# Key sums in one chain with one VectorE addition, and the router's rank products issued behind the next tile's transposes

## The chip, the cores and the metric

The kernel runs on one core of a Trainium2 chip (trn2). The time is that of one execution of the whole program on the device, in microseconds; smaller is better. A core has engines that each work through a queue of their own, in order: TensorE (PE; its weight loads are shown as PEld), VectorE (DVE), ScalarE (ACT), GpSimd (POOL) and SyncE (SP), which here only issues transfers. They wait for one another through semaphores. TensorE writes to the PSUM banks, and the other engines read these and the on-chip memory SBUF.

## The reference, cut to what matters

Two layers of gated cross-attention with a mixture of experts behind each. The change touches the router of the first mixture and the softmax of the second attention.

```python
def _L0_ffn_ref(x, router_w, wg, wu, wd):
    logits = jnp.einsum('bsh,eh->bse', x, router_w)
    ...
    idx = jnp.argmax(logits, axis=-1).reshape(-1)
    for e in range(E):
        ...
        out = out + jnp.where((idx == e)[:, None], y, 0.0)
...
def _L1_xattn_ref(query, key_value, Wq, bq, Wk, bk, Wv, bv, Wo, bo):
    scores = jnp.einsum('bhsd,bhtd->bhst', Q, K) * scale
    attn = jax.nn.softmax(scores, axis=-1)
    ctx = jnp.einsum('bhst,bhtd->bhsd', attn, V)
    ...
x = x + jnp.tanh(g_xattn[0]) * _L0_xattn_ref(_layernorm(x, axis=-1), ctx_2048, mask_BxS2_bk0)
x = x + jnp.tanh(g_ffn[0]) * _L0_ffn_ref(_layernorm(x, axis=-1), ...)
x = x + jnp.tanh(g_xattn[1]) * _L1_xattn_ref(_layernorm(x, axis=-1), ctx_2048, ...)
x = x + jnp.tanh(g_ffn[1]) * _L1_ffn_ref(_layernorm(x, axis=-1), ...)
```

Each softmax needs, for every query, the sum of the exponentials over its 1024 keys. Each token of the first mixture goes to one of 8 experts, so a kernel can sort the tokens by expert: it needs each token's expert and its rank among the tokens of that expert.

## The kernel before

The program runs through stages: the first attention with the router (44 to 314 us of the profile), the sorted first mixture (to about 440), the second attention (to about 1256) and the second mixture (to the end). In the stages that the change touches the order of instructions is written out by hand: each engine executes its own in the order of the program's text.

**The router's stage** runs over 16 tiles of 128 tokens, three or four tiles in flight (the loop at line 619). In iteration n, `turn_p(n)` transposes the probabilities of tile n in eight TensorE products, which ScalarE copies out (`a_prT`); `some_weights` prepares a piece of the experts' weights, once or twice per iteration (a `tot` product on TensorE in `weight_scale`, two long VectorE instructions on `w_all`, and two long ScalarE ones); `route_1(n-1)` normalises a row tile for the router; `scores(n+1)`, `turn_x(n+2)`, `softmax(n+1)` and `prepare(n+3)` follow; then `route_3(n-2)` makes the logits (`b_lgp`) and, in a row of small VectorE instructions, the one-hot expert of each token, `oh_all`; `readout(n)` and `finish(n)` close the attention of tile n (`a_o`, and its addition into `x` at line 493); `route_2(n-1)` transposes and quantises the row; and `route_4(n-2)` closes the iteration, before the loads and masks of the next batch. `route_4` (line 561) multiplies `oh_all` with a triangle of ones, and the running sum of earlier one-hots with ones, into one PSUM bank, `b_rkp` (lines 566 and 570): this is each token's rank. GpSimd adds the running sum, five small VectorE instructions from line 586 work out the row's place, and GpSimd issues the scatter of the row (line 595). The bank `lg` is shared by the logits and the rank products.

**The second attention** runs over 16 groups g (4 batches by 4 groups of four heads). A group has U = 16 units t = 16 g + k; unit k is chunk c = k // 2 of 128 keys and pair p = k % 2 of two heads. `score_pairs(t)` does two things at once. For the unit t + 21 it makes scores with queries down the partitions (`c_s`, line 1126), whose maxima VectorE takes (`c_mxn`, line 1143). For unit t it makes transposed scores with the maxima already subtracted (`c_t`, lines 1121 and 1132), which ScalarE exponentiates into a tile `e` (line 1141, 128 keys x 2 heads x 512 queries, nine buffers). The banks for `c_s`, `c_t` and the projections come from one ring of seven. Four units later `weigh` multiplies with the values (`c_o`).

The sum over keys goes three ways. `add_chunks(t)` adds the `e` tiles of one pair element by element, on GpSimd: of the first four chunks into one accumulator, and of the last four into another, so four accumulators and 12 additions per group (chunks 0 and 4 only start a pair, no instruction). `sum_chunks(g, h)` multiplies the two accumulators of half h by ones (four products, line 1209), which gives the sums over the partitions' keys; it is issued eight units after the end of its half, that is in unit 15 of the group for h = 0 and in unit 7 of the next for h = 1. The first half is copied out by ScalarE into `c_rec` (line 1218), and the second is added to it by VectorE (line 1220). `divide` takes reciprocals in four pieces on VectorE and multiplies on GpSimd (`c_oT`, line 1228).

In unit 9 of a group (where `(t + LEAD) % U == 0`) the loop first issues the previous group's `divide`, then in groups 5, 7, 9, 11 and 13 the four row statistics of `ln_part`, then in groups 2, 6 and 10 the queries' projection, and `project_k` (line 1051): sixteen records of TensorE, during which no new scores arise. In unit 10 `split_maxima` reduces the maxima on VectorE (`c_mm`) and splits them into three parts on GpSimd (`c_nm`, `c_pc`); `turn_maxima` transposes these in unit 14. In groups 4, 8 and 12 the values' projection (`c_vp`) comes in unit 4.

Of the kernel before, what the change touches and what calls it, by code (L numbers as in the profile page):

```python
# [14 lines left out]
ALU = mybir.AluOpType  # L15
# [12 lines left out]
def flamingo_kernel(  # L28
# [26 lines left out]
    nc = tc.nc  # L55
# [6 lines left out]
    NM = M // P  # L62
# [115 lines left out]
    NQ = B * NT  # L178
# [122 lines left out]
    with ExitStack() as st:  # L301
# [163 lines left out]
        def turn_p(n):  # L465
            pr = pr_of[n][0]
            prT = wk.tile([P, NM, P], FP, tag="prT", name=f"a_prT_{n}")
            for h in range(NM // 4):
                tp = ps_p.tile([P, 4, P], FP, tag="tp", name=f"a_tp2_{n}_{h}")
                for c in range(4):  # L470
                    nc.tensor.transpose(tp[:, c, :], pr[:, bass.ts(h * 4 + c, P)], ident)
                nc.scalar.copy(prT[:, bass.ts(h, 4), :], tp)  # L472
            prT_of[n] = prT
# [87 lines left out]
        def route_4(n):  # L561

            nonlocal oh_sum
            oh = oh_all[:, n, :]
            rk_ps = ps_1.tile([P, 512], FP, tag="lg", name=f"b_rkp_{n}")
            nc.tensor.matmul(
                rk_ps[:, 0:E], lhsT=earlier, rhs=oh, start=True, stop=(n == 0)
            )
            if n:
                nc.tensor.matmul(  # L570
                    rk_ps[:, 0:E], lhsT=ones_b, rhs=oh_sum, start=False, stop=True
                )
            if n == NQ - 1:
                cnt_ps = rk_ps[:, E : 2 * E]
                nc.tensor.matmul(cnt_ps, lhsT=ones_b, rhs=oh_sum, start=True, stop=False)
                nc.tensor.matmul(cnt_ps, lhsT=ones_b, rhs=oh, start=False, stop=True)
                nc.vector.tensor_copy(cnt, cnt_ps)
            else:
                total = sst.tile([P, E], BF, tag="oh_sum", name=f"b_ohsum_{n}")
                if n:  # L580
                    nc.gpsimd.tensor_tensor(total, oh_sum, oh, ALU.add)
                else:
                    nc.gpsimd.tensor_copy(total, oh)
                oh_sum = total
            mine = sst.tile([P, E], FP, tag="mine", name=f"b_mine_{n}")
            nc.vector.tensor_tensor(mine, rk_ps[:, 0:E], oh, ALU.mult)
            nc.vector.tensor_reduce(rank_all[:, n : n + 1], mine, AX.X, ALU.add)
            place = sst.tile([P, E], FP, tag="place", name=f"b_place_{n}")
            nc.vector.tensor_tensor(place, room_e, oh, ALU.mult)
            plc = sst.tile([P, 1], FP, tag="plc", name=f"b_plc_{n}")  # L590
            nc.vector.tensor_reduce(plc, place, AX.X, ALU.add)
            to = sst.tile([P, 1], U32, tag="to", name=f"b_to_{n}")
            nc.vector.tensor_tensor(to, plc, rank_all[:, n : n + 1], ALU.add)
            row = route_of.pop(n)[1]
            nc.gpsimd.indirect_dma_start(
                out=rows_d[:, :], out_offset=bass.IndirectOffsetOnAxis(ap=to[:, :], axis=0),
                in_=row[:, :], in_offset=None,
            )
# [19 lines left out]
        h = 0  # L618
        for n in range(-2, NQ):
            if 0 <= n < NQ:  # L620
                turn_p(n)
            if n >= 0:
                some_weights(h)
                h += 1
            if 0 <= n - 1 < NQ:
                route_1(n - 1)
            if 0 <= n + 1 < NQ:
                scores(n + 1)
            if n + 2 < NQ:
                turn_x(n + 2)  # L630
            if n == -2:
                for q in range(4):
                    weight_load(q, nc.scalar)
                nc.scalar.activation(gates, graw, AF.Tanh)
                nc.scalar.preload_act_table_set("natural_log_exp_and_others")
            if n == -1:
                set_valid(0)
            if 0 <= n + 1 < NQ:
                softmax(n + 1)
            if n + 3 < NQ:  # L640
                prepare(n + 3)
            if n >= 0 and n % 4 != 3:
                some_weights(h)
                h += 1
            if n == NQ - 1:
                break
            if 0 <= n - 2 < NQ:
                route_3(n - 2)
            if 0 <= n < NQ:
                finish(n, readout(n))  # L650
            if 0 <= n - 1 < NQ:
                route_2(n - 1)
            if 0 <= n - 2 < NQ:
                route_4(n - 2)
            if n >= -1 and (n + 5) % NT == 0 and n + 5 < NQ:
                load_x((n + 5) // NT)
                load_memT((n + 5) // NT)
                load_mem((n + 5) // NT)
            if n >= 0 and (n + 4) % NT == 0 and n + 4 < NQ:
                set_mask((n + 4) // NT)  # L660
            if n >= 0 and (n + 3) % NT == 0 and n + 3 < NQ:
                set_valid((n + 3) // NT)

        n = NQ - 1
# [22 lines left out]
        acc_all = memp.tile([P, 4, 2, S], FP, tag="mem", name="c_acc")  # L687
# [267 lines left out]
    with ExitStack() as st:  # L955
# [22 lines left out]
        NG = B * NK  # L978
        U = 16
# [9 lines left out]
        for i in range(2):  # L989
            t = big.tile([P, NT, 4, HD], BF, tag=f"pc{i}", name=f"c_pc_{i}")  # L990
# [5 lines left out]
        mxn_of, mT_of, e_of, acc_of, ou_of, rec_of = {}, {}, {}, {}, {}, {}  # L996
# [171 lines left out]
        def weigh(g, c, h):  # L1168
# [10 lines left out]
            if c == NM - 1 and h == 1:  # L1179
                ou_of[g] = wk.tile([P, S], FP, tag="ou", name=f"c_ou_{g}", bufs=1)  # L1180
                nc.scalar.copy(ou_of[g], o_bank)  # L1181

        def add_chunks(t):

            g, k = divmod(t, U)
            c, p = divmod(k, 2)
            if c % 4 == 0 or (g == NG - 1 and c >= NM - 2):
                return

            eng = nc.vector if g == NG - 1 and t % 2 else nc.gpsimd  # L1190
            if c % 4 == 1:
                acc = acc_all[:, (2 * (c // 4) + p) % 4]
                acc_of[g, c // 4, p] = acc
                eng.tensor_tensor(acc, e_of[t - 2], e_of[t], ALU.add)  # L1194
            else:
                acc = acc_of[g, c // 4, p]
                eng.tensor_tensor(acc, acc, e_of[t], ALU.add)  # L1197

        def sum_chunks(g, h):
            ps = ps_s.tile([P, S], FP, tag="s", name=f"c_sum_{g}_{h}")  # L1200
            terms = [(acc_of[g, h, 0], acc_of[g, h, 1])]
            if g == NG - 1 and h == 1:

                terms += [
                    (e_of[g * U + 2 * c], e_of[g * U + 2 * c + 1]) for c in (NM - 2, NM - 1)
                ]
            for n, term in enumerate(terms):
                for i in range(4):
                    nc.tensor.matmul(  # L1209
                        ps[i * HD : (i + 1) * HD, :], lhsT=ones[:, 0:HD],  # L1210
                        rhs=term[i // 2][:, i % 2, :],
                        start=(n == 0), stop=(n == len(terms) - 1),
                    )
            if h == 1 and g == NG - 1:
                return ps
            if h == 0:
                rec_of[g] = wk.tile([P, S], FP, tag="rec", name=f"c_rec_{g}", bufs=1)
                nc.scalar.copy(rec_of[g], ps)
            else:
                nc.vector.tensor_tensor(rec_of[g], rec_of[g], ps, ALU.add)  # L1220

        def divide(g, q):
            rq = rec_of[g][:, bass.ts(q, P)]
            nc.vector.reciprocal(rq, rq)
            if q == NT - 1:
                oT = big.tile([P, S], FP, tag="oT", name=f"c_oT_{g}", bufs=5)
                eng = nc.vector if g == NG - 2 else nc.gpsimd
                eng.tensor_tensor(oT, ou_of.pop(g), rec_of[g], ALU.mult)
                oT_of[g] = oT
# [123 lines left out]
        for t in range(-LEAD, NG * U + LAG):  # L1353

            for j in range(NT):
                d = t + LEAD + NT + 1 - j
# [3 lines left out]
                d = t + LEAD + NT - j  # L1360
                if d % (NK * U) == 0 and 1 <= d // (NK * U) < B:
                    turn_q(d // (NK * U), j)
            if (t + LEAD) % U == 0 and 0 <= t + LEAD < NG * U:
                g = (t + LEAD) // U
                if g >= NK:
                    for q in range(NT):
                        divide((t - 24) // U, q)
                if t in stats_at:
                    tag, b = stats_at[t]
                    for j in range(NT):  # L1370
                        ln_part(b, j, tag)
                if g % NK == 0:
                    project_q(g // NK)
                if g >= NK:
                    project_k(g, 0)
                    project_k(g, 1)
# [51 lines left out]
                b, j = divmod(d, NT)  # L1428
                tp_of[d] = turn_d(ps_s, "s", b, j, xn_of.pop((b, j)), None)
            d = t - 2 * LAG  # L1430
            if 0 <= d < NG * U - 1 and d % 8 == 7:
                sum_chunks(d // U, d % U // 8)

            if (t + LEAD) % (NK * U) == (NK - 1) * U and 0 <= t:
# [162 lines left out]
```

## Time and profile before

| what | value |
|---|---|
| median of 3 runs | 1709.49 us (1706.15 to 1712.39) |
| the profiled execution | 1704.83 us, of which 1703.1 us are the span of its instructions |
| TensorE busy | 1644.9 us (97%) |
| VectorE busy | 845.9 us (50%) |
| ScalarE busy | 663.1 us (39%) |
| GpSimd busy | 630.8 us (37%) |
| router's stage, 44 to 314 us: TensorE, VectorE | 258.7 and 220.5 of 270 us |
| second attention, 440 to 1256 us: TensorE, VectorE, GpSimd | 806.7, 492.1 and 510.8 of 816 us |
| `c_sum` products by ones (line 1209) | 272 records, 592 ns each; 8 records for a half |
| GpSimd additions `c_acc` (lines 1194 and 1197) | 184, of 2.39 us |
| VectorE reciprocals `c_rec` (line 1224) | 60, of 0.91 us |
| rank products `b_rkp` (lines 566 to 576) | 33, of 166 ns |

The granted clock of TensorE was 0.998 over the span. The products of a half run beside one another on parts of the array, so a half takes less than its records' sum. A matrix product in 32-bit numbers shows as two records. The profile's lines give, in this order, the start, the length, the engine, the line and the operation, the output and inputs, and in brackets the engine's idle time before the instruction with what ended it.

### The profile page before, as it was taken

How to read it: one execution, taken by the hardware profiler on the slowest of the kernel's cores; microseconds unless marked ns; L12 is line 12 of the kernel's file. 1: busy time of each engine (PE TensorE's matmuls, PEld its weight loads, DVE VectorE, ACT ScalarE, POOL GpSimd, SP SyncE). 2: the span in 40 equal slices, each digit the busy share in tenths (PEclk: the TensorE clock that was granted, in tenths of full speed). 3: DMA queues.
4: the chain of work that ended last, by engine and by line, in shares of the span. 5: the costliest groups of instructions: out<-in, count | busy, mean ns of one | idle time of the engine just before them, and what ended most of it. 6: DMA issues, size and time to landing. Idle time of an engine off the chain costs nothing.

```text
span 1703.1 us, 22403 instructions
## 1 busy us (share of the span) xinstructions
PE 1644.9 (97%) x8853; PEld 808.5 (47%) x8853; DVE 845.9 (50%) x1750; ACT 663.1 (39%) x1168; POOL 630.8 (37%) x597
## 2 busy tenths in 40 slices
PE   6999999888999999999999999999999999999999
PEld 3554545344433334333343333433365676567766
DVE  3888886565587562675726757267641001100110
ACT  3655663386136353353533535336720111011100
POOL 1011111563249494574955848458800000000000
PEclk9999999999999999999999999999999999999999
DMA  9466533496010000010000100001045354534530
GB/s 347 158 238 229 191 117 115 155 323 197 25 50 1 1 13 13 1 50 1 14 13 1 51 1 1 1 1 51 1 175 214 132 195 169 189 130 148 205 123 25
DMA packets 76360, 173.12 MB, mean 102 GB/s; under 512 B 4512, under 2 KB 5552, under 8 KB 76256
## 3 DMA queue, kind: packets, MB, share of 16 engines
q1 hardware_dynamic: 62176, 128.07, 21.5%
q0 software_dynamic: 8368, 33.02, 5.9%
q10 hardware_dynamic: 5712, 10.62, 1.7%
q8 instruction: 69, 1.13, 0.3%
q14 instruction: 35, 0.29, 0.1%
HBM read 153.06 MB, written 18.62 MB: 101 GB/s over the span
## 4 chain that ended last, share of the span: by engine, by line
PE 81%; DVE 11%; ACT 2%; DMA 2%; issue 2%; POOL 1%; SPq 0%; ACTq 0%; DVEq 0%; POOLq 0%
PE d_h L1510 13%; PE d_o L1529 13%; PE c_s L1126 12%; PE c_o L1173 8%; PE c_vp L1068 6%; PE c_k L1051 5%; PE c_t L1121 5%; PE c_q L1029 3%; PE a_o L479 3%; PE a_s L444 2%; PE c_out L1081 2%; PE c_t L1132 2%; PE c_sum L1209 2%; DMA b_wt<-tern_d,widx 1%; DVE w_all L412 1%
## 5 line engine op out<-in xcount | busy, mean ns | idle before, releaser
L1143 DVE TENSOR_REDUCE c_mxn<-c_s 128x1 f32<-128x512 f32 x512 | 328.4, 685 | 239.3 <-PE c_s L1126 237.4
L1141 ACT ACTIVATE c_e<-c_t 128x512 f32<-128x512 f32 x512 | 276.9, 596 | 205.1 <-PE c_t L1132 203.0
L1197 POOL TENSOR_TENSOR c_acc<-c_acc,c_e 128x1024 f32<-128x1024 f32 x122 | 287.8, 2390 | 95.6 <-ACT c_e L1141 95.2
L1126 PE MATMUL c_s<-c_kT,c_qT 32*128 32x512 f32 x1024 | 302.0, 639 | 0.0
L1132 PE MATMUL c_t<-c_qT,c_kT 32*128 32x512 f32 x1024 | 256.9, 596 | 0.0
L1529 PE MATMUL d_o<-d_w,d_hT 128*128 128x512 f32 (+1 forms) x544 | 221.1, 567 | 0.0
L1510 PE MATMUL d_h<-d_xnT,d_w 128*128 128x256 f32 x992 | 215.4, 379 | 0.0
L1510 PEld LDWEIGHTS d_h<-d_xnT,d_w 128*128 128x128 f32 x992 | 188.5, 190 | 28.6 <-issue 3.4
L1516 ACT ACTIVATE d_hT<-d_h,b_t 128x256 f32<-128x256 f32 x128 | 60.6, 473 | 350.2 <-PE d_h L1510 350.2
L1534 DVE TENSOR_TENSOR d_o<-d_o,d_b 128x512 f32<-128x512 f32 x14 | 9.8, 700 | 346.9 <-PE d_o L1529 346.9
L1173 PE MATMUL c_o<-c_e,c_v 128*32 128x256 f32 x2048 | 160.9, 390 | 0.5 <-ACT c_ou L1181 0.5
L1529 PEld LDWEIGHTS d_o<-d_w,d_hT 128*128 128x128 f32 x544 | 103.4, 190 | 113.5 <-issue 111.5
L1194 POOL TENSOR_TENSOR c_acc<-c_e,c_e 128x1024 f32<-128x1024 f32 x62 | 147.3, 2397 | 18.6 <-ACT c_e L1141 18.6
L1173 PEld LDWEIGHTS c_o<-c_e,c_v 128*32 128x32 f32 x2048 | 41.7, 108 | 177.6 <-issue 163.6
L444 PE MATMUL a_s<-memT,a_xnT 128*128 128x512 f32 x256 | 116.5, 609 | 0.7 <-ACT a_xnT L436 0.7
L479 PE MATMUL a_o<-mem,a_prT 128*128 128x512 f32 x256 | 114.6, 598 | 0.2 <-ACT a_prT L472 0.2
L1126 PEld LDWEIGHTS c_s<-c_kT,c_qT 32*128 32x128 f32 x1024 | 95.9, 183 | 12.4 <-DVE c_mxn L1143 7.7
L1121 PE MATMUL c_t<-c_mT,c_ones_bf 3*128 3x512 bf16 x512 | 97.4, 384 | 1.9 <-DVE c_rec L1220 1.4
L536 POOL TENSOR_SCALAR b_rx<-b_amc 128x1 f32<-128x1 f32 x16 | 3.5, 221 | 242.0 <-DVE b_amc L525 242.0
L1503 POOL DMA_DIRECT2D d_b<-in_b x8 | 4.4, 556 | 218.5 <-DVE d_o L1534 198.0
L1051 PE MATMUL c_k<-c_memT,w_all 128*128 128x512 f32 x192 | 85.3, 597 | 0.0
L1068 PE MATMUL c_vp<-w_all,c_memT 128*128 128x512 f32 x192 | 83.2, 594 | 0.0
(296 smaller groups left out, 1952.1 us busy)
## 6 DMA issues: line engine op xcount, KB each, us to landing
d_w<-in_w SPq DMA_DIRECT2D x63, 1024.0 KB
w_all<-in_wuT SPq DMA_DIRECT2D x7, 1024.0 KB
w_all<-in_wdT SPq DMA_DIRECT2D x7, 1024.0 KB
memT<-in_memT SPq DMA_DIRECT2D x3, 2048.0 KB
mem<-in_mem SPq DMA_DIRECT2D x3, 2048.0 KB
tern_d<-t ACTq DMA_DIRECT2D x24, 256.0 KB
w_all<-in_wgT SPq DMA_DIRECT2D x6, 1024.0 KB
c_memT<-in_memT SPq DMA_DIRECT2D x3, 2048.0 KB
```

The costliest lines, as they stand in the source:

```text
L479: nc.tensor.matmul(o_ps, lhsT=prT[:, c, :], rhs=mem_t[:, c, :], start=(c == 0), stop=(c == NM - 1),)
L1051: nc.tensor.matmul(ps, lhsT=wk_t[:, k, bass.ts(o, P)], rhs=memT_of[b][:, k, bass.ts(n, HALF)], start=(k == 0), stop=(k == NK - 1),)
L1068: nc.tensor.matmul(ps, lhsT=memT_of[b][:, k, bass.ts(c, P)], rhs=wv_t[:, k, :], start=(k == 0), stop=(k == NK - 1),)
L1121: nc.tensor.matmul(t_of[i], lhsT=ones_bf[r, :], rhs=mT_of[g][r, :], start=True, stop=False)
L1126: nc.tensor.matmul(s_of[i], lhsT=qT_of[gs][r, bass.ts(j, P)], rhs=kT_of[gs][r, bass.ts(n, HALF)], start=True, stop=True,)
L1132: nc.tensor.matmul(t_of[i], lhsT=kT_of[g][r, bass.ts(c, P)], rhs=qT_of[g][r, :], start=False, stop=True,)
L1141: nc.scalar.activation(e_t[:, i % 2, :], t_of[i], AF.Exp)
L1143: nc.vector.tensor_reduce(mxn_of[gs][:, j, i, n : n + 1], s_of[i], AX.X, ALU.max)
L1173: nc.tensor.matmul(o_bank[i * HD : (i + 1) * HD, hs], lhsT=v_all[:, c, bass.ts(o * 4 + i, HD)], rhs=e_of[g * U + 2 * c + i // 2][:, i % 2, ...
L1197: eng.tensor_tensor(acc, acc, e_of[t], ALU.add)
L1510: nc.tensor.matmul(ps[:, 0 : B * CAP], lhsT=w1c[n][:, k, bass.ts(fo, P)], rhs=xnT[:, k, :, bass.ts(e, CAP)], start=(k == 0), stop=(k == NK ...
L1529: nc.tensor.matmul(ps[:, o], lhsT=hT[:, f, bass.ts(half, P)], rhs=w2c[n][:, fo, o], start=(f == 0), stop=(f == NF - 1),)
```

## The change

Two parts, independent of each other.

The rank products: `route_4(n-2)` at the end of iteration n becomes `route_4(n-3)` in the next iteration, directly behind `turn_p(n)`. The calls behind the loop are as before.

The key sums: for groups 2 to 13 (`one_chain`) the two halves become one chain. There is one accumulator for each pair, which begins with chunk 1 and takes the other chunks in turn; the four slots of `acc_all` are used by even and odd groups in turn. Chunk 4 is now added: for the second pair by GpSimd (unit 9), for the first pair by VectorE, as one instruction in unit 9 behind the reciprocals of `divide`. `sum_chunks` is called once, in unit 7 of the next group, and its result is copied by ScalarE. Groups 0, 1, 14 and 15 stay as they are.

```diff
         for n in range(-2, NQ):
             if 0 <= n < NQ:
                 turn_p(n)
+            if 0 <= n - 3 < NQ:
+                route_4(n - 3)
...
             if 0 <= n - 1 < NQ:
                 route_2(n - 1)
-            if 0 <= n - 2 < NQ:
-                route_4(n - 2)
...
+        one_chain = range(2, NG - 2)
+
         def add_chunks(t):
 
             g, k = divmod(t, U)
             c, p = divmod(k, 2)
-            if c % 4 == 0 or (g == NG - 1 and c >= NM - 2):
+            if c == 0 or (g == NG - 1 and c >= NM - 2):
                 return
+            if c == 4 and (g not in one_chain or p == 0):
+                return
 
             eng = nc.vector if g == NG - 1 and t % 2 else nc.gpsimd
-            if c % 4 == 1:
+            if g in one_chain:
+                if c == 1:
+                    acc_of[g, 1, p] = acc_all[:, 2 * (g % 2) + p]
+                    eng.tensor_tensor(acc_of[g, 1, p], e_of[t - 2], e_of[t], ALU.add)
+                else:
+                    acc = acc_of[g, 1, p]
+                    eng.tensor_tensor(acc, acc, e_of[t], ALU.add)
+            elif c % 4 == 1:
                 acc = acc_all[:, (2 * (c // 4) + p) % 4]
...
-            if h == 0:
+            if h == 0 or g in one_chain:
                 rec_of[g] = wk.tile([P, S], FP, tag="rec", name=f"c_rec_{g}", bufs=1)
                 nc.scalar.copy(rec_of[g], ps)
...
                 if g >= NK:
                     for q in range(NT):
                         divide((t - 24) // U, q)
+                    acc = acc_of[t // U, 1, 0]
+                    nc.vector.tensor_tensor(acc, acc, e_of[t - 1], ALU.add)
                 if t in stats_at:
...
-            if 0 <= d < NG * U - 1 and d % 8 == 7:
+            if 0 <= d < NG * U - 1 and (d % U == 15 or d % U == 7 and d // U not in one_chain):
                 sum_chunks(d // U, d % U // 8)
```

## The prediction

> **What bounds the kernel now.** I read the chain of waits first, then the list of waits, then the timeline of each engine around the edits. The chain is followed back from the last instruction; its engine shares, and then some of its pieces in order of time (start, length, engine, tile, line):
>
> ```profile
> PE 81%; DVE 11%; ACT 2%; DMA 2%; issue 2%; POOL 1%; SPq 0%; ACTq 0%; DVEq 0%; POOLq 0%
> ...
> 220.74 0.24 DVE oh_all L559
> 221.03 0.17 PE b_rkp L566
> 221.22 0.93 PE a_tp L471 x8
> ...
> 237.48 0.75 DVE x L493
> ...
> 640.59 0.86 PE c_sum L1209 x8
> 641.44 0.32 PE c_t L1121 x2
> ```
>
> So the attention stage (440 to 1256 us) is bound by TensorE, and the key sums stand in its chain at 0.86 us per half. In the router stage (44 to 314 us) the chain changes hands: VectorE's `oh_all` holds TensorE (221.03), and TensorE's readout holds VectorE (237.48). The list of waits from 60 to 300 us gives both sides (who waited for whom: us in total, times, longest):
>
> ```profile
> PE b_rkp L566 <- DVE oh_all L559: 9.6, 8, 2.2
> ...
> DVE x L493 <- PE a_o L479: 10.5, 6, 5.1
> ```
>
> **The router's move.** Nothing is added or removed: the two or three rank products (166 ns each), `total` on GpSimd, five small VectorE instructions (about 0.16 us each) and the scatter from GpSimd's queue are issued one iteration later, behind the eight transposes of `turn_p`. On VectorE they pass `set_mask` or `set_valid` only (0.69 and 1.2 us, one tile in four each); on GpSimd nothing stands between; SP issues none of it, and the loads of the next batch, which now stand ahead of it in the program, don't wait for it. TensorE no longer waits for `oh_all` before `turn_p`: the probabilities that it transposes were ready 5.7 us earlier (at 215.4 for 221.08). `b_mine` reads the product 2.3 us after it ran, and gives 1.1 us of that to the transposes, so no new wait.
>
> What it is worth: VectorE is the tighter engine from tile 3 to tile 12. It waited for the readout at 93.7, 165.5 and 237.5 us, 1.13 us each. Before these, TensorE had lost 1.38, 2.21 and 2.20 us at the rank products, so all three waits close: 3.4 us. From 221 us to 309 us TensorE is busy almost without a break (16.8 to 17.0 us of every 17 up to 289) and decides. There it can start earlier by VectorE's 2.26 us and by 1.92 us more: the next thing in its queue, the `tot` product at 221.99, needs ScalarE's sum, ready at 220.07. That is 4.2 us, with 0.27 us that it loses at 255 makes **4.5 us** gained; the low end is VectorE's 3.4, the high end 5.5 if `tot` isn't in the way.
>
> **The sums: what goes.** Groups 2 to 13 lose the first `sum_chunks`: four products with 0.86 us in the chain, 12 x 0.86 = **10.3 us** gained. With it go 12 additions into `c_rec` on VectorE (0.69 us) that were hidden in its idle time, and ScalarE's copy (0.585 us) moves from unit 15 to unit 7 of the next group, where ScalarE has 1.5 us free. Costed at nothing.
>
> **The sums: what comes.** GpSimd does 13 additions of 2.36 us per group where it did 12. The new one is unit 9's, and stands where GpSimd now waits for the maxima before `c_nm` or for statistics (1.8 to 1.9 us in groups 3 and 7, 4.7 to 20 in the others), while `c_nm` and its pieces are done 1.9 us or more before the transposes that read them. I cost it at nothing but 0.15 us where it has no idle time; without that cover it would be 2.36 us of lag per group.
>
> VectorE does 12 links. Each is queued in front of the next maxima, and of `ln_part` in groups 5, 7, 9, 11 and 13. The cover is the keys' projection, 7.06 us of TensorE without a new score. Group 7 shows how full it is (start, length, idle before and releaser):
>
> ```profile
> 828.16 9.29 POOL L1197 TENSOR_TENSOR c_acc<-c_acc,c_e 128x1024 f32<-128x1024 f32 x4
> ...
> 830.79 3.38 DVE L1224 RECIPROCAL c_rec<-c_rec 128x128 f32<-128x128 f32 x4
> ...
> 837.13 0.18 DVE L129 BATCH_NORM_AGGREGATE mv_d<-bn_d 128x2 f32<-128x6 f32 x1
> 838.39 1.29 DVE L1143 TENSOR_REDUCE c_mxn<-c_s 128x1 f32<-128x512 f32 x2 [1.08 <-PE c_s L1126]
> ```
>
> The projection starts at 830.17; I count from there. Reciprocals end at 4.0, statistics take 3.15 more, and the next scores are there at 8.23: only 1.08 us are free in groups with statistics, 4.2 in the others. When VectorE is late at 8.23, TensorE is late too: the ring has seven banks and a unit takes four, so the second score product of one unit needs the bank of the first one of the unit before. At 839.14 that product starts, 0.05 us after the reduction of 838.39 has ended. There is no slack, and each microsecond of lateness is a microsecond of the stage.
>
> **The link's price.** Nothing of this form runs alone on VectorE. A 128x512 addition takes 667 ns there and a 128x128 one 292, so 0.98 ns an element, and 1024 elements 1.2 us. Beside GpSimd it is dearer:
>
> ```profile
> 1217.81 3.14 DVE L1194 TENSOR_TENSOR c_acc<-c_e,c_e 128x1024 f32<-128x1024 f32 x1 [10.98 <-ACT c_e L1141]
> ...
> 765.55 2.79 DVE L166 TENSOR_SCALAR c_xn<-x,mv_c,rstd_c 128x512 f32<-128x512 f32 x1
> ...
> 1223.15 3.34 POOL L1194 TENSOR_TENSOR c_acc<-c_e,c_e 128x1024 f32<-128x1024 f32 x1
> ```
>
> Both read as taking turns: `c_xn` needs 0.55 us alone, and 2.79 is that and one GpSimd addition; 3.14 is the rest of one and 1.2; GpSimd's 3.34 is its own 2.36 and about 1. So I price the link at 1.2 us, after whatever GpSimd has begun. The bounds are 1.2 us with no waiting, and 3.2 throughout.
>
> The Trainium skill (SBUF — State Buffer, "SBUF: two separate sides") says that VectorE with two operands in SBUF and GpSimd hold a common port exclusively for a whole instruction and that bandwidth isn't split. By that rule the sum is the one with turns below; by a reading of the 3.14 us row as shared speed it is the one with 3.2. The page speaks against this change: the link sits beside GpSimd's own additions.
>
> Start of the link: after the reciprocals (4.0) and after GpSimd's unit-6 addition; unit 8's exponentials are done at 0.7. GpSimd's unit-10 addition waits for the link, but comes to it at 14.5 at the earliest. GpSimd's ends of units 6 and 7 in the timeline are 0.9 and 3.2 (groups 5, 9), 1.35 and 3.66 (11), 2.1 and 4.4 (13), -0.65 and 1.7 (4, 8, 12), 4.97 and 7.3 (3, 7). Groups 3, 7 and 11 have GpSimd busy without a break since before the removed product, so counted from a projection that comes 0.86 us earlier they lie 1.0 later (with the 0.15). Then:
> - 5, 9: link 4.0 to 5.2, statistics to 8.35: late 0.1 each
> - 11: after unit 7 at 4.65, to 5.85, statistics to 9.0: 0.8
> - 13: after 4.4, to 5.65, to 8.8: 0.6
> - 3: unit 6 at 6.0, GpSimd goes on with unit 7 to 8.3, link to 9.5: 1.25
> - 7: the same and 3.15: 12.65, late 4.4
> - 4, 8, 12 end at 5.2; in 2, 6, 10 the queries (13.9 us) come first: 0
>
> That is 7.25 us lost. With no waiting for turns it is 2.5 (2.1 of it in group 7), with 3.2 throughout 13.5 (2.1 in each of 5, 9, 11, 13, 1.0 in 3, 4.1 in 7).
>
> **Sum.** -4.5 - 10.3 + 7.25 = -7.5 us. On the profiled execution (1704.83 us, of which 1703.1 span) that is 1697.3. The runs' median, 1709.49, lies 4.7 above it, so the forecast for the median is 1702. The link's bounds give -12.3 and -1.3; with the router's, -13.3 and -0.2, so 1696 to 1709. The runs themselves spread by 3 us to either side.
>
> **Rivals.** A measurement of this kernel can tell about 0.3% (5.1 us) from no change, so faster means under 1704.4.
> - *The links hide nearly all* (GpSimd isn't late in 3 and 7, or the order of turns favours VectorE): stalls 0 to 2.5, -12.3 to -14.8, about 1696. For it: the 20 us idle of GpSimd in groups 2, 6, 10 just before. Against: its additions run unbroken from 811.88 to the link.
> - *Shared speed*: 3.2 us per link, -1.3, 1708. For it: three VectorE rows at 3.14 to 3.20. Against: `c_xn`, and GpSimd's oT multiplication beside most links lasts 1.27 only.
> - *The router's move does nothing*, since ScalarE or the sums hold TensorE at `turn_p` instead: -3.0, 1706.5. Against: 1.92 us of slack at `tot`.
> - *Slower: GpSimd falls behind.* Its additions (2.36) are longer than a unit (1.77); the mechanism is that unit 9's addition isn't absorbed before `c_nm` and the lag is carried to the next link. One addition of lag puts the lateness at 1.7 (5, 9), 3.0 (11), 2.9 (13), 3.6 (3) and 6.7 (7), 19.6 together: +4.8, 1714; two make +19, 1728. It decides from one addition of lag at unit 6. For it: groups 3 and 7 carry row additions too. Against: the idle time before `c_nm` in every group, and 22 us during the values' projections.
>
> **Chances.** Forecast 0.45 (nearly all of it faster), hidden links 0.15 (faster), shared speed 0.20 and router without effect 0.08 (within 0.3%, some faster), GpSimd behind 0.12 (slower). Faster 0.58, within 0.3% 0.30, slower 0.12. The range, 1694 to 1711, holds the bounds with the runs' spread and leaves out most of the slower case; the forecast's own is 1697 to 1708.
>
> **What would show it.** Right: no wait of `b_rkp` for `oh_all`; the rank stage's end some 4.5 us earlier; `c_sum` with 96 of its 272 records gone (8 for each of twelve halves); links of 1.2 us in groups 4, 5, 8, 9 and about 3.5 where an addition is under way; the gap between projection and next unit longer in group 7 by about 4 us and by about 1 in 3. Wrong: links of 3.2 us everywhere, `c_nm` or `c_sum` waiting for GpSimd's additions, or a new wait of TensorE at `tot` or `b_lgp`.

## The result, and the profile after

The changed kernel is slower: a median of 1718.77 us (1714.28 to 1721.7, six runs) against 1708.37 us (1706.15 to 1712.39, six runs) for the kernel before, a ratio of 1.0056 with a 95% interval of 1.004 to 1.0073. The profiled execution took 1714.8 us, of which 1713.0 us are its span (1703.1 before). The forecast was 1702 us, and its range ended at 1711.

The head of the page of the changed kernel, with the shares of its chain:

```profile
span 1713.0 us, 22252 instructions
...
PE 1644.8 (96%) x8757; PEld 809.1 (47%) x8757; DVE 858.1 (50%) x1750; ACT 662.4 (39%) x1168; POOL 668.1 (39%) x609
...
PEclk9999999999999999999899999999999999999999
...
PE 80%; DVE 11%; DMA 3%; ACT 2%; POOL 2%; issue 2%; SPq 0%; ACTq 0%; DVEq 0%; POOLq 0%
```

TensorE has 96 records fewer and is busy for as long as before (1644.8 us for 1644.9): something made its remaining products slower. The 8 in the clock row is the place, in the middle of the attention stage. The list of waits of the changed kernel (who waited for whom: us in total, times, longest) has a line of 13.3 us, the first one here, that the list before has not:

```profile
PE c_s L1126 <- DVE c_mxn L1143: 13.3, 2, 8.2
DVE x L493 <- PE a_o L479: 9.4, 6, 5.1
PE b_rkp L566 <- DVE oh_all L559: 6.7, 5, 2.2
```

The links of the changed kernel, all twelve in one line (shortest, median and longest in ns):

```profile
L1381 DVE TENSOR_TENSOR c_acc<-c_acc,c_e x12: 1158/1160/8096, 573.7 to 1170.6; 128x1024 f32<-128x1024 f32 x12
```

Eight take 1.16 us, about what the prediction gave a link that waits for nothing; group 13's takes 1.63 and group 11's 2.05. The two of groups 3 and 7 take 8.09 and 8.10 us. The timeline of VectorE, then of GpSimd, around the first of them (start, length, idle before and its releaser):

```profile
620.73 3.38 DVE L1236 RECIPROCAL c_rec<-c_rec 128x128 f32<-128x128 f32 x4
626.37 8.09 DVE L1381 TENSOR_TENSOR c_acc<-c_acc,c_e 128x1024 f32<-128x1024 f32 x1 [2.26 <-POOL c_acc L1202]
634.38 1.87 DVE L1143 TENSOR_REDUCE c_mxn<-c_s 128x1 f32<-128x512 f32 x3
...
619.37 9.26 POOL L1202 TENSOR_TENSOR c_acc<-c_acc,c_e 128x1024 f32<-128x1024 f32 x4
628.60 1.26 POOL L1240 TENSOR_TENSOR c_oT<-c_ou,c_rec 128x512 f32<-128x512 f32 x1
629.82 1.25 POOL L248 TENSOR_TENSOR x<-x,b_back 128x512 f32<-128x512 f32 x1
631.04 2.33 POOL L1202 TENSOR_TENSOR c_acc<-c_acc,c_e 128x1024 f32<-128x1024 f32 x1
```

The profile shows the link as begun as soon as GpSimd's unit-6 addition, the third of its row of four, is done. Unit 7's addition, the multiplication for `oT`, an addition into `x` and unit 9's addition then pass one behind the other without a gap and at their usual lengths. GpSimd's row ends at 633.37, and the link ends 1.09 us later, which is nearly the whole of its usual 1.16: it did next to nothing until then. The reductions behind it free the banks that TensorE waits for.

Busy times in six stretches of the changed kernel: group 3 from the start of the keys' projection to the end of TensorE's wait, the stretch behind it and the next; then, for group 7, the wait alone and the two stretches behind it. Each line gives the stretch and its length, then the busy us and the number of instructions of TensorE, its weight loads, VectorE, ScalarE and GpSimd, then the granted clock, the DMA share and GB/s:

```profile
620.11:635.11 15.00, 9.95 (x43) 3.84 (x39) 12.74 (x9) 3.14 (x6) 13.26 (x7) 0.95 0.06 17
635.11:640.34 5.23, 5.23 (x24) 1.45 (x24) 2.11 (x5) 1.08 (x2) 1.76 (x7) 0.50 0.01 3
640.34:645.00 4.66, 4.66 (x52) 1.79 (x54) 3.62 (x6) 3.05 (x6) 4.52 (x3) 1.00 0.00 0
843.50:851.74 8.24, 0.01 (x1) 0.00 (x0) 8.10 (x11) 0.00 (x0) 3.56 (x3) 0.60 0.00 0
851.74:858.79 7.05, 7.05 (x38) 2.40 (x42) 3.31 (x6) 2.56 (x6) 2.47 (x12) 0.50 0.01 2
858.79:864.00 5.21, 5.21 (x56) 1.59 (x48) 3.48 (x6) 2.87 (x6) 5.05 (x4) 1.00 0.00 0
```

TensorE waits 5.06 us in group 3 and 8.23 us in group 7, and resumes at a clock of 0.50, for another 5.23 and 7.05 us: 24 records in 5.23 us, then 52 in 4.66. The grant fell during the wait: by the trace's clock the stretches at half speed begin at 633.5 and 845.1 and last 6.83 and 13.65 us.

From the keys' projection beside the first link (583.6 us, 583.4 before) to the last `c_s` the attention stage takes 629.3 us instead of 619.6. The rank stage's last readout ends 1.2 us earlier than before (298.7 for 299.9), and the router's gain is down to 0.2 us when the first mixture's last product begins (413.2 for 413.4).

My theory after this reading: the two links that were shut out cost the waits, and the waits brought on the half clock. The rivals: GpSimd's thirteenth addition makes VectorE late in any group; the half clock comes by itself; the loss comes with the router's move; VectorE and GpSimd share speed, so that such a link costs 8 us wherever it starts.

### The profile page after: what moved, and what is told of

Its sections match the earlier page's. It is cut to its first block, busy times and chain, and to the rows that moved or that the text cites. A ratio compares the mean times of both kernels' runs of the same rounds, so it can differ in the third digit from the quotient of the medians.

```text
span 1713.0 us, 22252 instructions
## 1 busy us (share of the span) xinstructions
PE 1644.8 (96%) x8757; PEld 809.1 (47%) x8757; DVE 858.1 (50%) x1750; ACT 662.4 (39%) x1168; POOL 668.1 (39%) x609
## 3 DMA queue, kind: packets, MB, share of 16 engines
q8 instruction: 69, 1.13, 0.3%
## 4 chain that ended last, share of the span: by engine, by line
PE 80%; DVE 11%; DMA 3%; ACT 2%; POOL 2%; issue 2%; SPq 0%; ACTq 0%; DVEq 0%; POOLq 0%
PE d_h L1524 13%; PE d_o L1543 13%; PE c_s L1126 12%; PE c_o L1173 8%; PE c_vp L1068 6%; PE c_k L1051 5%; PE c_t L1121 4%; PE c_q L1029 3%; PE a_s L444 3%; PE a_o L479 3%; PE c_out L1081 2%; DMA b_wt<-tern_d,widx 2%; PE c_t L1132 2%; DVE w_all L412 1%; DVE w_all L413 1%
## 5 line engine op out<-in xcount | busy, mean ns | idle before, releaser
L1202 POOL TENSOR_TENSOR c_acc<-c_acc,c_e 128x1024 f32<-128x1024 f32 x132 | 310.0, 2377 | 165.1 <-ACT c_e L1141 164.9
L1126 PE MATMUL c_s<-c_kT,c_qT 32*128 32x512 f32 x1024 | 310.1, 646 | 13.3 <-DVE c_mxn L1143 13.3
L1132 PE MATMUL c_t<-c_qT,c_kT 32*128 32x512 f32 x1024 | 261.3, 605 | 0.0
L1132 PEld LDWEIGHTS c_t<-c_qT,c_kT 32*128 32x128 f32 x1024 | 82.4, 186 | 0.3
```

The lines of the kernel that those rows point to most:

```text
L1126: nc.tensor.matmul(s_of[i], lhsT=qT_of[gs][r, bass.ts(j, P)], rhs=kT_of[gs][r, bass.ts(n, HALF)], start=True, stop=True,)
L1132: nc.tensor.matmul(t_of[i], lhsT=kT_of[g][r, bass.ts(c, P)], rhs=qT_of[g][r, :], start=False, stop=True,)
```

## Experiments

Groups are counted by their sums, as in the prediction: the link of group g runs beside the keys' projection of group g + 2. Ratios are to the kernel before, measured beside each; the forecasts in the quoted expectations are in microseconds.

### One part alone

The kernel before with the router's move only:

```diff
+            if 0 <= n - 3 < NQ:
+                route_4(n - 3)
...
-            if 0 <= n - 2 < NQ:
-                route_4(n - 2)
```

> Only the router's move, the sums as before. My theory: little. After the change the rank products still wait for oh_all, since VectorE reaches it no earlier, and only the 0.93 us of transposes in front of them is taken out of each loss: the rank stage ends about 1.2 us earlier and the stage behind it gives that back to its own loads, so 1708 within 2 us, ratio 0.999 to 1.001. The prediction's step says 4.5 us faster, ratio 0.997. A rival that makes the move the loser (TensorE's stretch of half clock at 149 us comes with it and costs more than the move brings) says 1 to 3 us slower, ratio 1.001 to 1.002.

1705.92 us, ratio 0.9989 (0.9977 to 1.0001): 1.9 us faster, which can hardly be told from none, and not the 4.5 of the prediction. Its waits:

```profile
DVE x L493 <- PE a_o L479: 9.3, 6, 5.1
PE b_rkp L566 <- DVE oh_all L559: 6.8, 5, 2.2
```

Three of eight waits of `b_rkp` are gone, five are left, the longest as long as before. The move is no loser. The stretch of half clock at 149 us doesn't belong to it either: the next run, which has the router as it was, shows one too (151.8 us), and so does the run with the old router near the end (149.3).

The changed kernel with the router as it was:

```diff
-            if 0 <= n - 3 < NQ:
-                route_4(n - 3)
...
+            if 0 <= n - 2 < NQ:
+                route_4(n - 2)
```

> Only the key sums in one chain, the router as before. My theory: the whole loss is here. Two links of 8.1 us (groups 3 and 7), TensorE's waits of 5 and 8 us behind them and its half clock afterwards cost 19 us, ten groups gain 0.86 us each: 9 to 10 us slower, 1718, ratio 1.0055. If half of the loss came with the router's move it is 1713, ratio 1.003; the prediction's own sum for this part is 3 us faster, ratio 0.998.

1720.27 us, ratio 1.0069 (1.0055 to 1.0083). The whole loss is in the sums. With the move the ratio is 1.0056; as the two intervals overlap, these runs can't tell that the move makes the loss smaller.

### Groups 3 and 7 as before

The change without its links in groups 3 and 7 (the accumulators' slots are swapped from group 3 to 6 so that none is overwritten):

```diff
-        one_chain = range(2, NG - 2)
+        one_chain = [g for g in range(2, NG - 2) if g not in (3, 7)]
...
+            flip = 2 * (3 <= g < 7)
...
+                    if t // U in one_chain:
+                        acc = acc_of[t // U, 1, 0]
+                        nc.vector.tensor_tensor(acc, acc, e_of[t - 1], ALU.add)
```

> The change, but groups 3 and 7 keep two halves, so the two links that took 8.1 us are not there. My theory (only these two links meet a GpSimd that runs without a gap): ten links of 1.16 us, no wait of c_s for c_mxn over 2 us, and 10 x 0.86 = 8.6 us less than before: 1699 to 1701, ratio 0.995 to 0.996. Rival, GpSimd's thirteenth addition delays VectorE in any group: the long links move to the groups behind (4 and 8), and the time stays at 1712 or more. Rival, the half clock comes by itself at the same places: 4 to 7 us of it remain, 1704 to 1707.

1698.79 us, ratio 0.9954 (0.9939 to 0.9969): faster than both. Nine of its ten links take 1.16 to 1.64 us, the one of group 11 2.05 us. The line of 13.3 us is gone from its waits, and the attention stage shows no stretch of half clock. So the thirteenth addition is harmless in the ten groups that have it here, and without the two waits the half clock doesn't come in this stage.

### The link by GpSimd in groups 3 and 7

```diff
-            if c == 4 and (g not in one_chain or p == 0):
+            if c == 4 and (g not in one_chain or p == 0 and g not in (3, 7)):
                 return
...
-                    acc = acc_of[t // U, 1, 0]
-                    nc.vector.tensor_tensor(acc, acc, e_of[t - 1], ALU.add)
+                    if t // U not in (3, 7):
+                        acc = acc_of[t // U, 1, 0]
+                        nc.vector.tensor_tensor(acc, acc, e_of[t - 1], ALU.add)
```

> As the changed kernel, but in groups 3 and 7 the link is GpSimd's (a fourteenth addition, in its place in the row) and VectorE adds nothing there. My theory: the cause is VectorE's instruction that is shut out, so the 5 and 8 us waits of c_s for c_mxn go; but GpSimd comes to c_nm 4.1 us later than it does with two halves (two more additions of 2.36 us less 0.6 us idle), of which 1.9 us are free, so TensorE's transposes of the maxima wait about 2.2 us in each of the two groups, with a few us at half clock perhaps: 1701 to 1706. Rival, GpSimd's added work is what delays VectorE, whoever makes the link: one addition more makes it no better than the changed kernel, 1717 or more.

1701.15 us, ratio 0.9943 (0.9923 to 0.9964). More work for GpSimd, and yet faster: it is VectorE's instruction that costs, not GpSimd's load. The price that I foresaw in both groups, TensorE's wait for the pieces of the maxima, is there in group 7 alone (0.28 us in group 3), with a stretch of half clock (3.41 us) at its end:

```profile
845.49 0.61 PE L1161 MATMUL c_mtp<-ident_bf,c_pc 128*128 128x128 bf16 x4 [2.23 <-POOL c_pc L1154]
```

The stage's other stretch of 3.41 us is in group 11 (from 1046.7 us), where the link is still VectorE's: it takes 3.32 us there, and TensorE waits 1.13 us.

The same with GpSimd's additions of units 8 and 9 behind `c_nm` and its pieces in these groups:

```diff
-                add_chunks(t)
+                late = t // U in (3, 7)
+                if late and t % U == 10:
+                    add_chunks(t - 2)
+                    add_chunks(t - 1)
+                if not late or t % U not in (8, 9):
+                    add_chunks(t)
```

> As the run before, but in groups 3 and 7 GpSimd's additions of units 8 and 9 stand behind c_nm and its pieces. My theory: no wait of c_s or of the transposes of the maxima is left, all twelve halves are gone, and GpSimd's lag of some 5 us melts in the values' projections and the idle time behind: 1697, two us below the kernel with two halves in groups 3 and 7 (1698.8). Rival, the lag goes on to the exponentials (their buffers come free later) and TensorE: 1701 to 1706.

1696.0 us, ratio 0.9918 (0.989 to 0.9947). The wait for `c_pc` is gone, and GpSimd's lag reaches nobody. What is left is a wait of 1.1 us for `c_mxn` in group 11, where the link takes 3.29 us; no half clock follows it here.

### When the shut-out link ends

The link queued behind the statistics (`ln_part`) instead of in front of them:

```diff
-                    acc = acc_of[t // U, 1, 0]
-                    nc.vector.tensor_tensor(acc, acc, e_of[t - 1], ALU.add)
                 if t in stats_at:
...
+                if g >= NK:
+                    acc = acc_of[t // U, 1, 0]
+                    nc.vector.tensor_tensor(acc, acc, e_of[t - 1], ALU.add)
                 if g % NK == 0:
```

> As the changed kernel, but the link is queued behind the statistics, where a group has both (5, 7, 9, 11, 13). My theory: in group 7 the link ends when GpSimd's row ends, whenever it was begun, so it takes 8.1 less 3.2, about 5 us, the statistics pass inside GpSimd's row, TensorE's wait falls from 8.2 to 5.1 us and its stretch of half clock from 13.65 to 6.8: 4.2 to 4.9 us faster than the changed kernel, 1714. Rival, VectorE and GpSimd share speed over the whole row and the link needs its 8 us of it wherever it starts: link of about 8 us, 1718 or more.

1710.58 us, ratio 0.9996 (0.9973 to 1.0019). VectorE's timeline in group 7, then GpSimd's:

```profile
840.52 0.18 DVE L129 BATCH_NORM_AGGREGATE mv_d<-bn_d 128x2 f32<-128x6 f32 x1
840.62 7.25 DVE L1386 TENSOR_TENSOR c_acc<-c_acc,c_e 128x1024 f32<-128x1024 f32 x1
847.79 1.87 DVE L1143 TENSOR_REDUCE c_mxn<-c_s 128x1 f32<-128x512 f32 x3
...
843.23 1.25 POOL L248 TENSOR_TENSOR x<-x,b_back 128x512 f32<-128x512 f32 x1
844.45 2.33 POOL L1202 TENSOR_TENSOR c_acc<-c_acc,c_e 128x1024 f32<-128x1024 f32 x1
```

The link takes 7.25 us, neither the 5 nor the 8 that were expected: I had forgotten that VectorE was idle for 2.24 us before it, and the statistics fill these first. What decides is the end. It comes at 847.87, again 1.09 us behind the end of GpSimd's row (846.78), and in the changed kernel, where it began 0.8 us earlier, it came at 847.92. Statistics run at their usual 0.66 us beside GpSimd. The wait of `c_s` in this group falls from 8.23 to 5.03 us, the half clock from 13.65 to 10.24 us, of which some 7.1 us lie behind the wait in both kernels. From group 2 on the stage is 4.3 us shorter than in the profile of the changed kernel, 3.2 of it in group 7 and 0.8 in group 11; the two kernels' ratios put the gain at 10 us, with 5 us to either side.

The link ahead of the reciprocals in groups 3 and 7, so that `oT`'s multiplication can't be ready:

```diff
                 if g >= NK:
+                    acc = acc_of[t // U, 1, 0]
+                    if t // U in (3, 7):
+                        nc.vector.tensor_tensor(acc, acc, e_of[t - 1], ALU.add)
                     for q in range(NT):
                         divide((t - 24) // U, q)
-                    acc = acc_of[t // U, 1, 0]
-                    nc.vector.tensor_tensor(acc, acc, e_of[t - 1], ALU.add)
+                    if t // U not in (3, 7):
+                        nc.vector.tensor_tensor(acc, acc, e_of[t - 1], ALU.add)
```

> As the changed kernel, but in groups 3 and 7 the link stands ahead of the reciprocals, so that GpSimd's multiplication for oT, which needs them, isn't ready and GpSimd's row breaks after unit 7's addition. My theory: the link waits for that addition only and takes 3.4 to 3.5 us (2.3 and 1.16) in both groups; the reciprocals follow, VectorE is done 1.2 us earlier than in the changed kernel: 1715 to 1717. Rival, the price of a link belongs to the additions on GpSimd beside it (two of them still run at that time) and not to the break: 6 to 8 us as before, then the reciprocals behind it, and 1722 or more.

1714.17 us, ratio 1.0019 (0.9997 to 1.004). VectorE's timeline in group 3, then GpSimd's:

```profile
625.08 3.36 DVE L1380 TENSOR_TENSOR c_acc<-c_acc,c_e 128x1024 f32<-128x1024 f32 x1 [5.53 <-POOL c_acc L1202]
628.36 3.37 DVE L1236 RECIPROCAL c_rec<-c_rec 128x128 f32<-128x128 f32 x4
...
618.10 9.25 POOL L1202 TENSOR_TENSOR c_acc<-c_acc,c_e 128x1024 f32<-128x1024 f32 x4
631.88 1.26 POOL L1240 TENSOR_TENSOR c_oT<-c_ou,c_rec 128x512 f32<-128x512 f32 x1 [4.53 <-DVE c_rec L1236]
```

The link takes 3.36 us here and in group 7: GpSimd's row now breaks at 627.35, and 1.09 us later the link is done. The data are the same, and the link begins at the same point, when unit 6's addition ends; only what GpSimd had ready behind its next addition is different. Shared speed is out. VectorE is still late in both groups, as the reciprocals now follow the link: TensorE waits 3.55 and 6.76 us, with 6.83 and 10.24 us of half clock. In group 11 the link takes 3.29 us here; a wait of 1.1 us and 6.83 us of half clock go with it. So the kernel is no faster than the one before.

### A wait without a link

The kernel before, with statistics that nobody reads on VectorE, beside the projections of sums' groups 4, 8 and 12:

```diff
+                for _ in range({6: 16, 10: 20, 14: 12}.get(g, 0)):
+                    hold = stat.tile([P, 6], FP, tag="bn", name=f"hold_{g}_{_}")
+                    nc.vector.bn_stats(hold, xs[0][:, 0, :])
```

> The kernel before, in which VectorE does further statistics that nobody reads, 16, 20 and 12 times 0.63 us behind the reciprocals of groups 4, 8 and 12, beside the keys' projection; no link, no change of the sums. They hold TensorE by their length less the 4.2 us that are free there: 5.9, 8.4 and 3.4 us. My theory (a wait of TensorE of that length is followed by a stretch at half clock, whatever caused it): clock near 0.5 for some 3.4 to 14 us behind the longer ones, and 17.7 us of waiting plus 7 to 14 us, so 1733 to 1741. Rival, the half clock belongs to something else in the changed kernel: no such stretch, 1726.

1734.03 us, ratio 1.0156 (1.0134 to 1.0178), 26 us more. The waits are shorter than expected, 4.14, 6.52 and 1.77 us: one of these statistics takes 0.595 us in a row, and 5.4 us were free, not 4.2. Wait, stretch behind it and next stretch for group 4; then wait and stretch behind it for group 8:

```profile
695.26:699.40 4.14, 0.00 (x1) 0.00 (x0) 4.14 (x8) 0.00 (x0) 0.00 (x0) 0.88 0.00 0
699.40:705.23 5.83, 5.83 (x32) 1.66 (x32) 2.71 (x6) 1.48 (x3) 2.36 (x7) 0.50 0.01 3
705.23:711.00 5.77, 5.77 (x49) 2.22 (x42) 3.18 (x6) 2.86 (x6) 5.77 (x3) 1.00 0.00 1
914.79:921.31 6.52, 0.00 (x1) 0.00 (x0) 6.52 (x12) 0.00 (x0) 0.00 (x0) 0.66 0.00 0
921.31:927.09 5.78, 5.78 (x32) 1.66 (x32) 2.66 (x6) 1.44 (x3) 2.31 (x7) 0.50 0.00 0
```

Without any link the clock halves: for 6.83, 10.24 and 6.83 us, of which 5.83, 5.78 and 6.83 us lie behind the waits. The half lost in them makes 9.2 us; the waits make 12.4 us. Two more stretches of 3.41 us began some 72 us after the ends of the first two, behind waits of 1.6 us for `c_xn` that the kernel before has too, without half clock; 3.4 us more. Together 25.0 us, and the waits for `c_xn` are 2.2 us longer in all (6.3 for 4.1). Between the two profiled executions the stage, from group 2 on, grew by 28.4 us (648.1 for 619.6), so 1.2 are not accounted for; by the medians the loss is 26 us. Waits alone would be 14.6.

### The better kernel, and the router's move in it

The changed kernel once more, as the reference of the next three:

> The changed kernel itself once more, beside the next three on one chip, so that they can be compared with it: 1716 to 1720, two links of 8.1 us, waits of 5.1 and 8.2 us, the same stretches of half clock behind them.

1719.05 us, ratio 1.0057 (1.0043 to 1.0071). The links, waits and stretches of groups 3 and 7 are as expected. Two things are not: group 11's link takes 3.27 us in this profiled execution (1721.1 us), where it took 2.05 in the first one (1714.8). TensorE waits 1.08 us for it, a stretch of 3.41 us at half clock follows, and the group takes 67.81 us instead of 65.05. Another stretch of 3.41 us comes at 1243.2 us, at a wait of 1.43 us that has none in the first. The run with the sums alone shows the same two (67.82 us for group 11). So the links of groups 3 and 7 are not the whole loss in every execution, and the stage from group 2 on takes 629.3 us in one and 632.3 in the other.

GpSimd's late additions in groups 3, 7 and 11, against the kernel that has them in two groups (the same in the two other places):

```diff
-                late = t // U in (3, 7)
+                late = t // U in (3, 7, 11)
```

> The run with GpSimd's late additions in groups 3 and 7, now in group 11 too, where the link on VectorE took 3.3 us and TensorE waited 1.1 us for c_mxn. My theory: that wait goes, 1.3 to 2.1 us faster than with groups 3 and 7 alone, ratio 0.990 to 0.993 to the kernel before. Rival, GpSimd has no room for a fourteenth addition in group 11, which has no values' projections behind it: exponentials wait, 2 us slower or more.

1693.74 us, ratio 0.9915 (0.9901 to 0.9929): 15.2 us under the kernel before and 25.3 us under the changed one. No wait of `c_s` for `c_mxn` is left and no half clock in the attention stage. Against the kernel with two groups (0.9918) the step can't be told by the ratios; in the traces group 11 is 2.06 us shorter (64.24 for 66.30).

The same with the router as before:

```diff
-            if 0 <= n - 3 < NQ:
-                route_4(n - 3)
...
                 route_2(n - 1)
+            if 0 <= n - 2 < NQ:
+                route_4(n - 2)
```

> As the run with groups 3, 7 and 11, but the router as in the kernel before: what the router's move is worth in the better kernel. My theory: 1 to 2 us, so 1 to 2 us slower than its neighbour. Prediction: 4.5 us slower.

1697.01 us, ratio 0.9931 (0.9917 to 0.9944): the move is worth 3.3 us by the medians, between my theory and the predicted 4.5. The ratios' intervals allow anything from nothing to more than 4.5; but each of the five runs is slower than each of the five of its neighbour on the same chip (lowest 1695.71, highest there 1694.98). How much of it is the move's own stays open: this run's profile has two stretches of half clock in the rank stage (149.3 and 224.4 us) that neither its neighbour's nor, with the same router, that of the kernel before has.

The same with `route_4(n - 3)` behind `softmax(n + 1)`, so that the rank products come after the scores:

```diff
                 turn_p(n)
-            if 0 <= n - 3 < NQ:
-                route_4(n - 3)
...
                 softmax(n + 1)
+            if 0 <= n - 3 < NQ:
+                route_4(n - 3)
```

> As the run before, with the rank products put further back, behind the next tile's scores and its maximum, where oh_all is old. My theory (the rank product in the change still stood ahead of the scores and waited for oh_all there, which is why the move brought 1.2 us and not 4.5): no wait of b_rkp for oh_all, TensorE's scores 1 to 2 us earlier where it waited, VectorE's waits for the readout shorter, the rank stage's end 2 to 4 us earlier than in the change. If the stage behind it doesn't eat that, 2 to 4 us off the time too. Rival, VectorE alone sets the pace of that stage: its end moves by less than 1 us.

1730.03 us, ratio 1.0127 (1.0111 to 1.0142): 36 us slower than its neighbour, which neither theory foresaw. Its waits in the rank stage:

```profile
DVE x L493 <- PE a_o L479: 42.3, 12, 6.7
PE b_lgp L547 <- DVE b_mine L586: 23.7, 13, 3.4
```

No `b_rkp` waits for `oh_all` now, but the logits use the same bank `lg`, and `b_mine`, which empties it, stands behind the maximum on VectorE. TensorE waits there in 13 tiles, and several stretches at half clock follow. So this says nothing on whether VectorE alone sets that stage's pace; that stays open. In the change's place `b_mine` comes ahead of the maximum, and one such wait of 0.6 us is in its list.

## Why the prediction was wrong

By its own steps:

- **The link's price is the step that failed.** "So I price the link at 1.2 us, after whatever GpSimd has begun." In groups 3 and 7 it waited for what GpSimd had begun and for three more instructions (1.26, 1.25 and 2.33 us, 4.84 together). The prediction put its end 9.5 us after the projection's start; measured are 14.35 us (634.46 less 620.11), and 14.34 in group 7. Of the 4.85 us between, the three are as good as all. GpSimd's unit-6 addition, from which the link starts, was foreseen at 6.0 and came at 6.2. The upper bound, 3.2 us, came from rows of before in which a single GpSimd instruction goes first. The `c_xn` row of 2.79 us, read as taking turns, is one of them, and GpSimd's line beside it holds a hint:

```profile
756.44 9.32 POOL L1197 TENSOR_TENSOR c_acc<-c_acc,c_e 128x1024 f32<-128x1024 f32 x4
765.71 4.85 POOL L1194 TENSOR_TENSOR c_acc<-c_e,c_e 128x1024 f32<-128x1024 f32 x2
```

The addition that went ahead of `c_xn` (from 765.55) began at 765.71, 0.16 us after it. So what GpSimd "has begun" was not the limit even there: the addition that ran ended, and one more passed. None of the rows that the prediction shows has more than one passing, as groups 3 and 7 have; its own figures named the row that made this possible, GpSimd "busy without a break since before the removed product".
- **What it priced elsewhere held.** Groups 4, 5, 8 and 9 have links of 1.16 us and no wait; 13 has 1.63 us. Group 11 was put at 0.8 us, and cost 0.8 us in the first profile (65.05 us to the next projection, 64.24 without the link). That is in part luck: in the second profile of the same kernel it cost 3.6 us (67.81).
- **"Each microsecond of lateness is a microsecond of the stage" was too low.** The lateness itself had 1.06 us of slack (6.12 us late in group 3, a wait of 5.06), but each wait was paid again in clock: 5.23 and 7.05 us at 0.50 cost 2.6 and 3.5 us. No term of the sum held that. The attention stage of before has no wait of TensorE over 1.6 us, and so no such price in it; the hint stood in the first mixture, where 3.41 us at half clock (from 333.1) follow a wait of 2.2 us.
- **The halves: right in kind, the sum a little small.** 12 x 0.86 = 10.3 us were foreseen. From group 2 to the last `c_s` the kernel with late additions in groups 3, 7 and 11, which has no wait for `c_mxn`, takes 607.7 us and the one before 619.6: 12.0 us. The rest goes with TensorE's wait for `c_xn` in the queries' projections, 4.1 us in all before and 1.9 us after.
- **The router: right in kind, too large.** Not 4.5 us but 1.9 (-0.2 to 3.9) alone, and 3.3 in the better kernel; the rank stage ends 1.2 us earlier in the profile, not 4.5. "The next thing in its queue, the `tot` product", was wrong: the rank products stand ahead of `tot`, and still wait for `oh_all` five times, 6.7 us. Only the transposes (0.93 us) no longer stand behind that wait.
- **The sum.** The stage from group 2 on: -12.0 for the halves, +21.6 for the links (607.7 to 629.3), 9.7 us in all. Of the 21.6, waits are 13.3, half clock 6.1, group 11 0.8, and 1.4 are not traced. The prediction had -10.3 and +7.25. In the second profile of the changed kernel the stage is 3.0 us longer still, nearly all of it in group 11.
- **The rivals.** "GpSimd falls behind" named 1714 and the right sign, but by luck: GpSimd wasn't behind, and one addition more on it was faster. The prediction missed the case in which GpSimd is in time and leaves no gap.

The page SBUF — State Buffer of the Trainium skill ("SBUF: two separate sides") says that whichever of the two instructions starts first holds the pair of ports for its length. That fits the whole block of the link, and not its length: the three instructions that passed it started 2.2 to 4.7 us after it had begun to wait.

## What to carry to other kernels

A VectorE addition with both operands in SBUF can be held until the end of GpSimd's unbroken row, as in groups 3 and 7, and not only by the one instruction that runs. It needn't be (group 13), but a price that must hold takes the end of the row: look for the next idle time of GpSimd, and where there is none before the deadline, give the work to GpSimd itself. A wait of TensorE by a few microseconds is to be priced at more than its length, since here the clock halved with it (5.1 us cost 7.7, 8.2 cost 11.8). Where an edit pays in ten places and costs in two, take it out of the two: here that turned 10 us lost into 9 us gained, and giving the costly additions to GpSimd, with two of its own put behind the maxima, into 15.

## What the runs showed of the hardware

- GpSimd's queue can pass a waiting VectorE instruction several times. In all four profiled executions that had the link behind the reciprocals or statistics in groups 3 and 7 (the changed kernel twice, the sums alone, the link behind the statistics) it lost three hand-overs in a row: 8.09 or 8.10 us, and 7.25 where it began later. `c_xn` in the kernel before lost one (2.79 us, at 765.55) and went ahead of the next addition. In group 13 the link won the first (1.63 us). In group 11 the changed kernel showed both, 2.05 us in one execution and 3.27 in another; there the reciprocal that ends just as the link begins also releases GpSimd's next instruction. What decides a hand-over stays open. That GpSimd's instruction was released before VectorE's asked is not it alone: in group 3 the exponentials for unit 9's addition ended (629.60) after the link had begun (626.37), and the addition still went first.
- Stretches at half clock come in multiples of 3.41 us in these traces (but for the last, which the end of the program cuts short). Behind the waits listed next they begin inside the wait or within 0.3 us of its end; behind shorter ones the next began up to 2.2 us after it. Waits of 5.06, 8.23, 4.14, 6.52 and 1.77 us had stretches of 6.83, 13.65, 6.83, 10.24 and 6.83 us; waits of 1.1 to 1.6 us had none in most cases, 3.41 us in some and 6.83 us once. Length alone doesn't decide: the kernel before waits 2.21 us at 149.1 without a stretch, and 2.2 us at 332.2 with one of 3.41. The page TensorE: Matmul & The Clock Gate ("What's actually happening") gives a free-running window of 3.4 us and half rate after an idle one; the multiples agree, and the wait of 1.77 us shows that a wait shorter than a window can be enough.
